# Flamingo block on one core: another order of the first two groups of rows

## The chip, the cores and the metric

The kernel runs on one core of a Trainium2 chip. The core has a matrix engine (PE, TensorE) with its weight loads (PEld), three engines for elementwise work (DVE or VectorE, ACT or ScalarE, POOL or GpSimd) and a queue engine (SP) that issues most transfers. Each engine takes its instructions in the order in which the program issues them, and waits on semaphores for what other engines and transfers produce. The metric is the device time of one execution in microseconds (us).

## The reference

Four batches of 2048 rows x of 512 columns; per batch a context of 77 rows of 384 columns. Everything is float32.

```
h  = layernorm(x);  q = h @ Wq;  k = ctx @ Wk;  v = ctx @ Wv      # 16 heads of 64
a  = softmax(q @ k.T / 8) @ v                                      # per batch and head
x  = x + tanh(g_xattn) * (a @ Wo + bo)
i  = argmax(log_softmax(logits) - log(-log(u)))                    # one of 8 weights
x  = x + tanh(g_ffn) * (layernorm(x) @ W[i] + b[i])
```

## The kernel before

**Weights are folded first.** Since a context has only 77 rows, q @ k.T is x @ M with M = centred Wq times K of a batch, and the attention's output is P @ VO with VO = V of a head times Wo. So per batch there is one M (512 x 1280, 16 heads by 80 padded keys) and one VO (1280 x 512). K (`project_k`, L274) and V (`project_v`, L278) come from the context, M from `m_head` (L298) and `build_m` (L310), VO from `build_vo` (L327), a pair of heads at a time. Batch 0's M stays in SBUF; the M of the other batches and every VO go to DRAM (`m_d`, `vo_d`) and are loaded when their batch comes (`load_m`, `load_vo`). A pair of VO takes six matmuls into six PSUM banks; `engines` in `build_vo` names the engine that copies each of them out ("D" DVE, "A" ACT, in turn) into one of five staging buffers `vo_st`, from which SP writes it to DRAM. Wo sits in the first part of the `vo` tile (L593), and three of the five staging buffers in its rest; the other two lie in the tile of Wq (L611).

**Rows go in 16 groups of 512.** Each group passes through scores (x @ M), softmax, attention (P @ VO), the residual, and the feed-forward with its own statistics. All products are done by a seven-product scheme (Strassen's, in Winograd's form): class `Seven` (L445). `product(s)` issues the matmuls of product s, `post(s)` takes the result out of PSUM: s = 0, 1, 2, 6 by a copy on ACT into `snap`, s = 3, 4, 5 by an addition on DVE (L486). A bank that collects several products is used again by a later product only after the post between them, so product 6 waits for post 4. The scheme needs sums of the blocks of each operand: `weight_sum` (L120) for M, VO and W; `Columns.sum` (L434) T1 to T4 of x's and P's columns, mostly on POOL. The scores of a group are three such runs: `s0` (two column pairs, snap), `s1` (two) and `s2` (one).

**Softmax.** DVE turns scores back to rows (`s_rows`, L512), takes a maximum per head group (`head_max`, L522, four of them), ACT does 64 exps of 128 x 77 (`exps`, L528), DVE sums (`head_sum`), POOL scales (`head_scale`, L542), and DVE turns P to columns (`p_columns`, L546, ten transposes). The layernorm of x enters as a scale of the exps: `Norms` (L358) with `stats` on DVE, `mean` and `var`, each a small DVE reduction (L374) followed by a small matmul (L375), and `rstd` with a power on POOL.

**Order by hand.** There is no scheduler: the program's text is each engine's order. The main loop (L756) runs for i = 1 to 15 and does the scores of group i, the attention of group i-1 with the exps of group i beside it, and the feed-forward of group i-1. Groups 0 and 1 have their scores written out ahead of it:

- L594 to L613, the setup: gates (L215: tanh of the gates, the choice of W[i]), then K and the centring of Wq per pair of heads, then M with V in its second and third quarter. Between them the statistics of group 0 and its columns. x is loaded behind all weights on SP.
- L649 to L697, scores of group 0. VO pairs 0 to 4 are made between its products: 0 and 1 in `s0`, 2 and 3 in `s1`, 4 at the end of `s2`. W[i] is gathered (L250) and centred (`centre_wf`, L621).
- L700 to L754, scores of group 1. VO 5 and 6 stand between its first products, VO 7 after the sixth; then `load_vo(0)`. Exps of group 0 and its sums are spread between. Only after all products come three VO weight sums on DVE and the ten transposes `p_columns(0, ...)` in two halves, then all ten `s_rows` of group 1.
- In the loop's first turn (i = 1) the attention of group 0 begins. There W[i] is scaled (`scale_wf`, L627, eight ACT instructions and four POOL sums) in its second step.

Of the kernel before, what the change touches and what calls it, by code (L numbers as in the profile page):

```python
# [8 lines left out]
F32 = mybir.dt.float32  # L9
# [5 lines left out]
P = 128  # L15
# [4 lines left out]
def flamingo_block_kernel(  # L20
# [33 lines left out]
    nc = tc.nc  # L54
# [60 lines left out]
    def flat(t):  # L115
        n = len(t.shape) - 1
        names = " ".join("abcdef"[:n])
        return t.rearrange(f"p {names} -> p ({names})")

    def weight_sum(w, n, engine=None):  # L120

        to, a, b_, op = ((5, 0, 3, ALU.subtract), (3, 3, 2, ALU.add), (4, 3, 0, ALU.subtract),
                         (6, 1, 4, ALU.subtract))[n]
        (engine or nc.gpsimd).tensor_tensor(flat(w[:, to]), flat(w[:, a]), flat(w[:, b_]), op)  # L124
# [12 lines left out]
        return wp.tile([P, NDC, T], F32, tag="xc", name=name, bufs=3)  # L137

    cT = wp.tile([P, NCC, B, JP], F32, tag="row", name="cT", bufs=3)
    cR = snap[:, : NCC * BJ].rearrange("p (c b j) -> p c b j", c=NCC, b=B)  # L140
    wv = snap.rearrange("p (c f) -> p c f", c=NCC)
    wk = m_f[:, 4 * 2 * KH * P :][:, : NCC * ID].rearrange("p (c f) -> p c f", c=NCC)
    t = wp.tile([P, NK * T + KH * T2], F32, tag="pT", name="wq")
# [16 lines left out]
    def load_w(t, w, h, queue):  # L160
        queue.dma_start(out=t[:, :, ts(h, ID // 4)], in_=w[:, ts(h, ID // 4)].rearrange("(c p) f -> p c f", p=P))

    nc.vector.memset(tq[:, 0], 0.0)
    idle = tq[:, 0].rearrange("p n t -> p (n t)")
    for _ in range(5):
        ps = bank("ps_w")
        nc.tensor.matmul(ps, idle[:, :P], idle, start=True, stop=True)
    load_ctx(0, nc.sync)
    load_ctx(2, nc.scalar)
    load_ctx(1, nc.sync)  # L170
    load_w(wk, Wk, 0, nc.scalar)
    load_w(wk, Wk, 1, nc.scalar)
    load_w(wk, Wk, 2, nc.sync)
    load_w(wk, Wk, 3, nc.sync)
    nc.gpsimd.memset(cT[:, :, :, J:], 0.0)
    for c in range(NCC):
        nc.vector.tensor_copy(cT[:, c, :, :J], cR[:, c])
    for p in range(NP):
        nc.sync.dma_start(out=wq[:, p, :], in_=WqT[ts(p, P), :])
    nc.gpsimd.dma_start(out=gg[:, 0:1], in_=g_xattn.partition_broadcast(P))  # L180
    nc.gpsimd.dma_start(out=gg[:, 1:2], in_=g_ffn.partition_broadcast(P))
    nc.gpsimd.dma_start(out=lg, in_=logits.partition_broadcast(P))
    nc.gpsimd.dma_start(out=uu, in_=u.partition_broadcast(P))
    for a in range(NA):
        nc.gpsimd.dma_start(out=bo_c[ts(a, 32)], in_=bo[ts(a, P)].rearrange("(q e) -> e q", e=32))
    for h in range(4):
        load_w(wv, Wv, h, nc.sync)
    load(0)
# [6 lines left out]
    for a in range(NA):  # L195

        for a2 in range(NA):
            nc.gpsimd.affine_select(
                out=jm[:, a, :], in_=jm[:, a, :], compare_op=ALU.not_equal, fill=0.125,
                base=-32 * a2, pattern=[[-1, 32]], channel_multiplier=1)  # L200

    def by_chunk(t):

# [60 lines left out]
    vT = [(vT_f[:, ts(p, BP)] if p < 7 else wf_f[:, ds(NP * BP, BP)]).rearrange(  # L264
        "p (r b k) -> p r b k", b=B, r=R) for p in range(NP)]

    def project(w, p):
        ps = bank("ps_kv")
        for c in range(NCC):
            nc.tensor.matmul(ps[:, :BP], w[:, c, ts(p, P)], cT[:, c].rearrange("p b j -> p (b j)"),  # L270
                             start=(c == 0), stop=(c == NCC - 1))
        return ps[:, :BP]

    def project_k(p):  # L274
        d = kT[:, p].rearrange("p b k r -> p (b k r)")
        nc.scalar.copy(d, project(wk, p))

    def project_v(p):  # L278
        d = vT[p].rearrange("p r b k -> p b k r")
        copy = nc.vector.tensor_copy if p % 2 else nc.scalar.copy  # L280
        copy(d, project(wv, p).rearrange("p (b k r) -> p b k r", b=B, r=R))


    wqp = [wp.tile([P, 2, NP, P], F32, tag="xc", name="wqp", bufs=3) for _ in range(2)]
# [2 lines left out]
    def centre_wq(p):  # L287
        nc.vector.tensor_reduce(wqm[:, p : p + 1], wq[:, p, :], AX.X, ALU.add)
        nc.vector.tensor_scalar(wqm[:, p : p + 1], wqm[:, p : p + 1], -1.0 / D, None, ALU.mult)
        for h in range(2):  # L290
            src = by_chunk(wq[:, p, :])[:, ts(h, 2)]
            dst = wqp[h][:, :, p, :].rearrange("p q (a e) -> p q a e", a=NA)
            if h:
                nc.gpsimd.tensor_scalar(dst, src, wqm[:, p : p + 1], None, ALU.add)
            else:
                nc.vector.tensor_scalar(dst, src, wqm[:, p : p + 1], None, ALU.add)
# [54 lines left out]

    def load_vo(bi):
        src = vo_d.rearrange("h (r b k) e -> (h r) b k e", b=B, k=NK)[:, bi]
        for (o, c), blk in BLK.items():
            nc.sync.dma_start(out=vo[:, blk], in_=src[:, ts(c, KH), ts(o, D // 2)])


    class Norms:  # L358
# [225 lines left out]
    def store(f, g0=0, n=NG, queues=(nc.sync,)):  # L584
        for a in range(NA):
# [2 lines left out]


    stages = [t[:, : (B - 1) * NK * P].rearrange("p (b k) -> p b k", b=B - 1) for t in  # L590
              (m_f[:, 4 * 2 * KH * P :], vo_f, vo_f[:, NP * D :],
               flat(wp.tile([P, HA, NG, JP], F32, tag="s", name="m_st")))]
    wo = vo_f[:, : NP * D].rearrange("p (n e) -> p n e", n=NP)  # L593
    norms[0] = Norms(0)  # L594
    gates()
    for p in range(NP):
        project_k(p)
        centre_wq(p)
    build_m(0, 0, NP // 2, stages[:2])
    norms[0].stats(xg[0], 0, 0, NG)  # L600
    build_m(0, NP // 2, NP, stages[:2], 0)
# [6 lines left out]
    build_m(2, NP // 2, NP, stages[2:])  # L608
    for n in range(1, 4):
        weight_sum(m, n, nc.gpsimd if n == 3 else nc.vector)  # L610
    for u_ in (vo_f[:, NP * D :], wq_f):  # L611
        for e in range(u_.shape[1] // (3 * D)):
            vo_st.append(u_[:, ts(e, 3 * D)].rearrange("p (c e) -> p c e", c=3))  # L613

# [12 lines left out]
    def scale_wf(wfr):  # L627
        for c in range(NDC):
            for o in range(2):
                nc.scalar.activation(chunked(wf[:, BLK[o, c // 2], c % 2, :]),  # L630
                                     by_chunk(wfr[:, c, :])[:, ts(o, 2)], AF.Copy, scale=tgf)
        for n in range(4):
            weight_sum(wf, n)

    def scores0(i):
        return Seven("ps_s", w_scores, xc[i], (0, 1), SNAP)
# [7 lines left out]
    def norm_step(n, s):  # L644
        if s < 4:
            (n.mean, n.spread, n.var, n.rstd)[s]()


    n = norms[0]  # L649
    s0 = scores0(0)  # L650
    for s in range(6):
        s0.product(s)
        if s == 0:
            wfr = gather()
        if s in (2, 5):
            build_vo(s // 3, "AD")
        s0.post(s)
    for k in range(2):
        s_rows(0, k, s0.chunk(0, k))
# [1 line left out]
    for s in range(7):  # L661
        s1.product(s)
        if s == 0:
            s1.post(0)
            s0.product(6)
            s0.post(6)
            for k in range(2):
                s_rows(0, KH + k, s0.chunk(1, k))
            sum_wf(wfr)
        else:  # L670
            norm_step(n, s - 1)
        if s in (2, 4):
            build_vo(1 + s // 2, "AD")
        if s == 3:
            x_columns(1)
        if 0 < s:
            s1.post(s)
        if s == 5:
            for k in range(2):
                s_rows(0, 2 + k, s1.chunk(0, k))  # L680
# [4 lines left out]
    for s in range(7):  # L685
        s2.product(s)
        s2.post(s)
        if s in (0, 2):
            n1.stats(xg[1], 0, 4 * s, 8)
        if s == 5:  # L690
            s_rows(0, 4, s2.chunk(0, 0))
            load(2)
            centre_wf(wfr)
            build_vo(4, "A")
    s_rows(0, KH + 4, s2.chunk(1, 0))
    for t in ("T1", "T2", "T3", "T4"):
        xc[1].sum(t)  # L697
# [4 lines left out]
    s1 = Seven("ps_s", w_scores, xc[1], (2, 3), pieces(spare, 0, 2))  # L702
    s2 = Seven("ps_s", w_scores, xc[1], (4,), SNAP1)
    head_max(0, 0)
    head_max(0, 1)
    for s in range(6):
        s0.product(s)
        s0.post(s)
        if s == 1:
            build_vo(5, "D")  # L710
            head_max(0, 2)
        if s == 3:
            build_vo(6, "D")
            head_max(0, 3)
        if s == 5:
            head_sum(0, 0)
            head_scale(0, 0)
        e = (0, 0, 8, 14, 20, 26, 32)
        exps(0, e[s], e[s + 1])
    build_vo(7, "D")  # L720
    load_vo(0)
    for s in range(7):
        s1.product(s)
        s2.product(s)
        if s == 0:
            s1.post(0)
            s2.post(0)
            s0.product(6)
            s0.post(6)
            head_sum(0, 1)  # L730
            head_scale(0, 1)
        norm_step(n1, s)
        if 0 < s:
            s1.post(s)
            s2.post(s)
        e = (32, 40, 48, 56, 64)
        if s < 4:
            exps(0, e[s], e[s + 1])
        if s == 2:
            head_sum(0, 2)  # L740
            head_scale(0, 2)
        if s == 4:
            head_sum(0, 3)
            head_scale(0, 3)
    weight_sum(vo, 0, nc.vector)
    p_columns(0, 0, 5)
    pT[0].sum("T1")
    weight_sum(vo, 1, nc.vector)
    weight_sum(vo, 2, nc.vector)
    p_columns(0, 5, NK)  # L750
    for sv, k0, nk in ((s0, 0, 2), (s1, 2, 2), (s2, 4, 1)):
        for half in range(2):
            for k in range(nk):
# [2 lines left out]
    for i in range(1, NGRP):  # L756
# [67 lines left out]
        for s in range(7):  # L824
# [12 lines left out]
            if 1 <= s:  # L837
                e = (0, 10, 20, 32, 44, 56, 64)
                exps(i, e[s - 1], e[s])
            if s == 0 and i == 1:  # L840
                weight_sum(vo, 3)
                pT[j].sum("T3")
            if s == 1 and i == 1:
                scale_wf(wfr)
            if s == 2:
                pT[j].sum("T4")
                if swap_m:
# [175 lines left out]
```

## Time and profile before

| what | us |
|---|---|
| median of 3 runs (1302.33 to 1303.58) | 1302.78 |
| the profiled execution | 1302.34 |
| its span, first to last instruction | 1300.4 |
| PE resumes after the statistics of group 0 | 33.27 |
| last matmul of M in the setup ends | 58.1 |
| group 0's scores, last product ends | about 106.4 |
| group 1's scores, last product ends | 148.57 |
| attention of group 0 begins | 151.26 |
| feed-forward of group 0 begins | 197.62 |

The page of the profile has the busy time of each engine and the span in 40 slices of 32.5 us. A timeline gives, for one engine, the start and length of instructions, merged where they follow each other, and in brackets the idle time before them with what ended it. A matmul of float32 shows as two records. Rows that serve below: a product of 4 matmuls in group 0's `s0` takes 1.73 us, an attention product (10 matmuls) 4.31, a VO pair 2.92 to 2.95; on DVE a head's maximum 1.44 and 0.17 for its scaling, a VO evacuation 0.66, a transpose 0.6 to 0.7; on ACT an exp 0.345, a VO evacuation 0.69; on POOL a sum of 128 x 1280 2.9, a head's scaling 2.27.

### The profile page before, as it was taken

The page shows a single profiled execution, that of the slowest core. Times are in us where ns is not written, and L with a number is a line of the kernel's source. Part 1 is how long each engine was busy: PE and PEld are TensorE (multiplying, and loading weights), DVE is VectorE, ACT ScalarE, POOL GpSimd, SP SyncE. Part 2 cuts the span into 40 slices and gives each one's busy share as a digit, 9 for nine tenths or more (in the row PEclk, how much of TensorE's full clock was granted, in tenths as well). Part 3 has the DMA queues.
Part 4 walks back from the last instruction along what each step waited for, and adds up shares of the span by engine and source line. Part 5 has one row for each costly group of instructions (what it writes and reads, how often), then busy time and mean ns, then how long its engine had stood idle before and what let it go on. Part 6 is the DMA issues. An engine that isn't in the chain of part 4 may idle for free.

```text
span 1300.4 us, 16961 instructions
## 1 busy us (share of the span) xinstructions
PE 1260.2 (97%) x5780; PEld 1068.9 (82%) x5780; DVE 884.8 (68%) x1823; ACT 651.6 (50%) x1766; POOL 894.2 (69%) x495
## 2 busy tenths in 40 slices
PE   9999869999999999999999999999999999999996
PEld 5666658888888888888888888888888888888885
DVE  6669776766667676766667676666767676666556
ACT  4436482644628273653728273563818264463822
POOL 5332478585977788585986788585985888585765
PEclk9999989999999999999999999999999999999998
DMA  9775310112305030022304120032304111010102
GB/s 237 254 254 160 116 33 1 37 29 81 65 1 121 26 65 1 18 48 81 66 1 106 41 55 12 3 64 74 73 1 99 48 35 31 1 33 1 33 1 65
DMA packets 95285, 80.28 MB, mean 62 GB/s; under 512 B 3920, under 2 KB 83152, under 8 KB 95200
## 3 DMA queue, kind: packets, MB, share of 16 engines
q1 hardware_dynamic: 92528, 76.61, 22.9%
q10 hardware_dynamic: 2064, 1.47, 0.4%
q0 software_dynamic: 608, 1.13, 0.4%
q8 instruction: 46, 0.75, 0.2%
q14 instruction: 39, 0.32, 0.1%
HBM read 44.07 MB, written 35.13 MB: 61 GB/s over the span
## 4 chain that ended last, share of the span: by engine, by line
PE 62%; ACT 14%; POOL 13%; DVE 6%; DMA 2%; issue 2%; SPq 0%; DVEq 0%; POOLq 0%; ACTq 0%
PE ps_s L463 36%; PE ps_a L463 16%; ACT s L532 12%; PE ps_f L463 7%; POOL xc L558 5%; POOL tq L437 4%; POOL s L543 4%; DVE sm L539 2%; PE ps_vo L336 1%; ACT snap L473 1%; PE ps_kv L270 1%; DMA xg<-in_x_dram 1%; DMA wq<-in_WqT_dram 1%; PE ps_m L301 1%; DVE s L515 1%
## 5 line engine op out<-in xcount | busy, mean ns | idle before, releaser
L463 PE MATMUL ps_a<-pT,vo 128*128 128x256 f32 x2240 | 491.2, 381 | 14.4 <-ACT snap L473 7.6
L463 PEld LDWEIGHTS ps_a<-pT,vo 128*128 128x128 f32 x2240 | 426.9, 191 | 75.3 <-POOL wf L124 7.9
L532 ACT ACTIVATE s<-s,nmx,up 128x77 f32<-128x77 f32 x1024 | 355.7, 446 | 6.0 <-DVE nmx L526 6.0
L463 PE MATMUL ps_s<-tq,m 128*128 128x256 f32 x1280 | 294.1, 380 | 0.2 <-DVE m L124 0.2
L437 POOL TENSOR_TENSOR pT<-pT 128x1280 f32<-128x1280 f32 x64 | 186.8, 2920 | 131.7 <-PE ps_a L463 111.3
L463 PEld LDWEIGHTS ps_s<-tq,m 128*128 128x128 f32 x1280 | 241.6, 190 | 35.0 <-issue 2.4
L469 ACT COPY snap<-ps_s 128x512 f32<-128x512 f32 (+1 forms) x188 | 94.4, 511 | 310.4 <-DVE t L417 124.2
L463 PE MATMUL ps_s<-xc,m 128*128 128x256 f32 x960 | 222.9, 381 | 0.6 <-DVE wq L339 0.6
L463 PEld LDWEIGHTS ps_s<-xc,m 128*128 128x128 f32 x960 | 180.8, 190 | 28.9 <-DVE wq L339 2.3
L543 POOL TENSOR_TENSOR s<-s,sm 128x1232 f32<-128x1232 f32 x64 | 145.2, 2268 | 73.9 <-DVE sm L540 64.6
L486 DVE TENSOR_TENSOR snap<-snap,ps_s 128x512 f32<-128x512 f32 (+1 forms) x141 | 83.6, 594 | 91.3 <-PE ps_s L463 91.3
L515 DVE STREAM_TRANSPOSE s<-snap 128x512 f32<-128x512 f32 x156 | 100.0, 686 | 49.3 <-ACT snap L469 47.4
L539 DVE TENSOR_REDUCE sm<-s 128x16 f32<-128x1232 f32 x64 | 91.7, 1432 | 56.8 <-ACT s L532 56.8
L463 PE MATMUL ps_f<-tq,wf 128*128 128x256 f32 x512 | 120.3, 383 | 8.0 <-POOL tq L437 8.0
L578 ACT ACTIVATE t<-t,rs 128x128 f32<-128x128 f32 x248 | 75.8, 390 | 98.7 <-POOL rs L409 98.7
L463 PEld LDWEIGHTS ps_f<-tq,wf 128*128 128x128 f32 x512 | 95.7, 190 | 27.5 <-POOL tq L437 15.2
L402 POOL TENSOR_TENSOR rs<-rs,neghalf 128x16 f32<-128x16 f32 x16 | 50.2, 3136 | 93.6 <-DVE rs L399 93.6
L552 DVE STREAM_TRANSPOSE pT<-s 128x512 f32<-128x512 f32 x160 | 101.0, 678 | 13.8 <-POOL s L543 13.8
L437 POOL TENSOR_TENSOR tq<-xc,tq 128x512 f32<-128x512 f32 x64 | 81.5, 1273 | 32.6 <-PE ps_f L463 25.6
L473 ACT ACTIVATE snap<-ps_a,bo_c 128x256 f32<-128x256 f32 x128 | 53.7, 470 | 90.0 <-PE ps_a L463 54.4
L437 POOL TENSOR_TENSOR tq<-xc 128x512 f32<-128x512 f32 x64 | 81.3, 1270 | 24.1 <-DVE xc L412 18.1
L524 DVE TENSOR_REDUCE ps_st<-s 128x16 f32<-128x1232 f32 x64 | 92.4, 1444 | 2.1
(121 smaller groups left out, 1200.9 us busy)
## 6 DMA issues: line engine op xcount, KB each, us to landing
xg<-in_x_dram SPq DMA_DIRECT2D x64, 256.0 KB, 5.6
out_dram<-y SPq DMA_DIRECT2D x60, 256.0 KB, 4.0
vo<-vo_d SPq DMA_DIRECT2D x16, 640.0 KB, 5.4
m<-m_d SPq DMA_DIRECT2D x12, 640.0 KB, 3.9
vo_d<-vo SPq DMA_DIRECT2D x10, 512.0 KB, 3.4
m_d<-vo SPq DMA_DIRECT2D x4, 960.0 KB, 8.0
vo_d<-wq SPq DMA_DIRECT2D x6, 512.0 KB, 2.8
wq<-in_WqT_dram SPq DMA_DIRECT2D x8, 256.0 KB, 8.1
```

Of the source, the lines that this page charges most:

```text
L437: (engine or nc.gpsimd).tensor_tensor(self.at[name], self.at[a], self.at[b_], op)
L463: nc.tensor.matmul(self.ps[r][:, n, :], self.w(blk, c, pair), self.cols(cname, c), start=(first and n == 0 and c == 0), stop=(c == h - 1), ...
L469: nc.scalar.copy(dst, self.ps[r])
L473: nc.scalar.activation(dst[:, n, :], self.ps[r][:, n, :], AF.Identity, scale=1.0, bias=self.bias[:, q : q + 1])
L486: nc.vector.tensor_tensor(c, c, self.ps[r], ALU.add)
L515: nc.vector.transpose(key_chunk(sc[i], k), cols.rearrange("p (g h r) -> p g h r", h=HA, r=R))
L524: nc.vector.tensor_reduce(mx, head(i, h), AX.X, ALU.max)
L532: nc.scalar.activation(head(i, h)[:, g, :], head(i, h)[:, g, :], AF.Exp, scale=norms[i].up[:, g : g + 1], bias=nmx[h][:, g : g + 1])
L539: nc.vector.tensor_reduce(sm, head(i, h), AX.X, ALU.add)
L543: nc.gpsimd.tensor_tensor(head(i, h), head(i, h), sums[h].unsqueeze(2).to_broadcast([P, NG, J]), ALU.mult)
L552: nc.vector.transpose(pT[i].all[:, k, :].rearrange("p (g h r) -> p g h r", h=HA, r=R), key_chunk(sc[i], k))
L578: nc.scalar.activation(ts_[f][:, g, :], ts_[f][:, g, :], AF.Copy, scale=rs[:, g : g + 1])
```

## The change

The diff moves work between the setup and the first two groups; the loop for groups 2 and on is the same.

1. Setup. The context is loaded raw into the tile that later stages M (`s_f`) instead of `snap`, and K reads it there with 77 columns per batch; only V reads the padded copy. POOL zeroes K's padding. Three warm-up matmuls instead of five. Wk's second quarter is issued on SP and its third on ACT, instead of the other way round. POOL's constants come ahead of the loads of the gates' inputs; the gates are computed after three of the eight K pairs; the bias `bo` is loaded after the loop.
2. VO. Pair 0 ahead of group 0's scores, 1 and 2 inside `s0`; 3 and 4 ahead of group 1's scores, 5 to 7 after its first three products. Evacuations "AAD" for pair 0, "AD" for 1 and 2, "ADD" for 3 to 7. The staging buffers in Wq's tile are used first. `load_vo(0)` follows VO 7, its blocks in another order.
3. W[i] is centred and scaled inside `s2` of group 0; three of its four sums are in `s1` and `s2` of group 1, the fourth in the attention.
4. The statistics of group 1 (`norm_step`) move from `s1`, `s2` to `s0` of group 1; exps and sums of group 0 are spread anew; eight of the ten `p_columns` and POOL's T1 move into steps 3 to 5 of `s1`, `s2`; the three VO weight sums move from DVE to POOL.

```diff
-    cR = snap[:, : NCC * BJ].rearrange("p (c b j) -> p c b j", c=NCC, b=B)
+    s_f = flat(wp.tile([P, HA, NG, JP], F32, tag="s", name="m_st"))
+    cR = s_f[:, : NCC * BJ].rearrange("p (c b j) -> p c b j", c=NCC, b=B)
...
-    for _ in range(5):
+    for _ in range(3):
...
     load_w(wk, Wk, 0, nc.scalar)
-    load_w(wk, Wk, 1, nc.scalar)
-    load_w(wk, Wk, 2, nc.sync)
+    load_w(wk, Wk, 1, nc.sync)
+    load_w(wk, Wk, 2, nc.scalar)
     load_w(wk, Wk, 3, nc.sync)
...
-    nc.gpsimd.dma_start(out=gg[:, 0:1], in_=g_xattn.partition_broadcast(P))
...
     nc.gpsimd.memset(jm, 0.0)
     for a in range(NA):
         for a2 in range(NA):
             nc.gpsimd.affine_select(
...
+    nc.gpsimd.dma_start(out=gg[:, 0:1], in_=g_xattn.partition_broadcast(P))
...
+    kT_f = kT.rearrange("p n b k r -> p n b (k r)")
+    nc.gpsimd.memset(kT_f[:, :, :, J:], 0.0)
...
     def project_k(p):
-        d = kT[:, p].rearrange("p b k r -> p (b k r)")
-        nc.scalar.copy(d, project(wk, p))
+        nc.scalar.copy(kT_f[:, p, :, :J], project(wk, p, cR).rearrange("p (b j) -> p b j", b=B))
...
     norms[0] = Norms(0)
-    gates()
     for p in range(NP):
+        if p == 3:
+            gates()
         project_k(p)
         centre_wq(p)
+    for a in range(NA):
+        nc.gpsimd.dma_start(out=bo_c[ts(a, 32)], in_=bo[ts(a, P)].rearrange("(q e) -> e q", e=32))
...
-    for u_ in (vo_f[:, NP * D :], wq_f):
+    for u_ in (wq_f, vo_f[:, NP * D :]):
...
     n = norms[0]
+    build_vo(0, "AAD")
     s0 = scores0(0)
...
         if s in (2, 5):
-            build_vo(s // 3, "AD")
+            build_vo(1 + s // 3, "AD")
         s0.post(s)
...
-        if s in (2, 4):
-            build_vo(1 + s // 2, "AD")
...
             n1.stats(xg[1], 0, 4 * s, 8)
+        if s == 1:
+            centre_wf(wfr)
+        if s == 3:
+            scale_wf(wfr)
         if s == 5:
             s_rows(0, 4, s2.chunk(0, 0))
             load(2)
-            centre_wf(wfr)
-            build_vo(4, "A")
...
     head_max(0, 0)
+    build_vo(3, "ADD")
     head_max(0, 1)
+    exps(0, 0, 6)
+    build_vo(4, "ADD")
+    head_max(0, 2)
+    exps(0, 6, 10)
+    e = (10, 16, 22, 28, 35, 42, 48)
     for s in range(6):
         s0.product(s)
         s0.post(s)
-        if s == 1:
-            build_vo(5, "D")
-            head_max(0, 2)
-        if s == 3:
-            build_vo(6, "D")
+        if s < 3:
+            build_vo(5 + s, "ADD")
+        if s == 0:
             head_max(0, 3)
-        if s == 5:
-            head_sum(0, 0)
-            head_scale(0, 0)
-        e = (0, 0, 8, 14, 20, 26, 32)
+        norm_step(n1, s)
         exps(0, e[s], e[s + 1])
-    build_vo(7, "D")
-    load_vo(0)
+        if s == 2:
+            load_vo(0)
+        if s in (2, 4):
+            head_sum(0, s // 2 - 1)
+            head_scale(0, s // 2 - 1)
+    e = (48, 53, 58, 64)
     for s in range(7):
         s1.product(s)
         s2.product(s)
...
-            head_sum(0, 1)
-            head_scale(0, 1)
-        norm_step(n1, s)
+            head_sum(0, 2)
+            head_scale(0, 2)
+            weight_sum(wf, 0)
+        if s < 3:
+            exps(0, e[s], e[s + 1])
+        if s == 1:
+            weight_sum(wf, 1)
+            weight_sum(wf, 2)
+        if s == 2:
+            head_sum(0, 3)
+            head_scale(0, 3)
+        if 3 <= s < 6:
+            p_columns(0, (0, 3, 5)[s - 3], (3, 5, 8)[s - 3])
+        if s == 4:
+            pT[0].sum("T1")
+        if s == 5:
+            weight_sum(vo, 0)
         if 0 < s:
             s1.post(s)
             s2.post(s)
...
-    weight_sum(vo, 0, nc.vector)
-    p_columns(0, 0, 5)
-    pT[0].sum("T1")
-    weight_sum(vo, 1, nc.vector)
-    weight_sum(vo, 2, nc.vector)
-    p_columns(0, 5, NK)
+    p_columns(0, 8, NK)
+    weight_sum(vo, 1)
+    weight_sum(vo, 2)
...
             if s == 0 and i == 1:
+                pT[j].sum("T3")
                 weight_sum(vo, 3)
-                pT[j].sum("T3")
-            if s == 1 and i == 1:
-                scale_wf(wfr)
+                weight_sum(wf, 3)
```

## The prediction, on record before the changed kernel ran

> **What bounds the kernel now.** I read the page's first two parts, then the matrix engine's (PE) timeline, then busy time by ten microseconds, then the timelines of the other engines and of the DMA queue SP, and last the order in which the changed kernel puts instructions on each engine.
>
> ```profile
> PE 1260.2 (97%) x5780; PEld 1068.9 (82%) x5780; DVE 884.8 (68%) x1823; ACT 651.6 (50%) x1766; POOL 894.2 (69%) x495
> PEclk9999989999999999999999999999999999999998
> ```
>
> PE is the bound, so only PE's own gaps can be won, and the clock fell only in the sixth slice of 32.5 us. From group 2 on PE hardly waits, and the change leaves those groups alone. The gaps stand before 210 us:
>
> ```profile
> 127.36 2.86 PE L463 MATMUL ps_s<-xc,m 128*128 128x256 f32 x12 [0.64 <-DVE wq L339]
> ...
> 151.26 5.18 PE L463 MATMUL ps_a<-pT,vo 128*128 128x256 f32 x20 [2.69 <-issue]
> 157.71 4.58 PE L463 MATMUL ps_a<-pT,vo 128*128 128x256 f32 x20 [1.26 <-POOL pT L437]
> 165.13 8.90 PE L463 MATMUL ps_a<-pT,vo 128*128 128x256 f32 x40 [2.84 <-POOL pT L437]
> 181.59 16.19 PE L463 MATMUL ps_a<-pT,vo 128*128 128x256 f32 x60 [7.57 <-ACT snap L473]
> 197.62 1.89 PE L463 MATMUL ps_f<-xc,wf 128*128 128x256 f32 x8
> ```
>
> Columns: start, length, what, and in brackets the wait. The waits shown make 15.0 us; 0.21, 0.36, 0.37 and 0.40 at 60, 81, 132 and 205 us make 16.3. After the 7.57 us wait the clock is low. One microsecond at a time:
>
> ```profile
> 176.00:177.00 1.00, 0.00 (x0) 1.00 0.00 0
> 177.00:178.00 1.00, 0.00 (x0) 0.72 0.00 0
> 178.00:179.00 1.00, 0.00 (x0) 0.50 0.00 0
> ...
> 186.00:187.00 1.00, 1.00 (x4) 0.50 0.00 0
> 187.00:188.00 1.00, 1.00 (x5) 0.66 0.00 0
> ```
>
> The fourth number is the granted clock: half from 177.4, 3.4 us after the last matmul (174.0), to 187.7. PE ran at half for 6.1 us (181.6 to 187.7) and lost 3.0. All told 19.3 us can be won, 1283 if nothing is added. DVE sits in front of these waits:
>
> ```profile
> 147.57 2.97 DVE L124 TENSOR_TENSOR vo<-vo 128x1280 f32<-128x1280 f32 x1
> 150.47 3.07 DVE L552 STREAM_TRANSPOSE pT<-s 128x512 f32<-128x512 f32 x5
> 153.47 5.54 DVE L124 TENSOR_TENSOR vo<-vo 128x1280 f32<-128x1280 f32 x2
> 158.93 3.07 DVE L552 STREAM_TRANSPOSE pT<-s 128x512 f32<-128x512 f32 x5
> ```
>
> Two of DVE's three VO weight sums (8.5 us in all) stand between the halves of P's transposes; the score transposes (6.2), the maxima, and on ACT exps and W's scaling (3.2) queue up behind.
>
> **The change part by part.** I follow one chain to the start of group 0's feed-forward, 197.62 before.
>
> *Setup: nothing.* Two warm-up matmuls go, keys read 308 columns instead of 320 (12/320 of 13.3 us, 0.5), Wk's second quarter moves to SP (0.64 wait at 12.5). All of it ends under one cover: DVE's statistics of x wait for x's landing at 29.5, and PE resumes at 33.27 behind them. The gates now stand in the key loop, and their small loads start some 5 us later on POOL (4.05 us of selects, plus memsets, come first). The logits took 7.8 us to land, so they come at about 15; gates 4.6, five centrings at 1.17 and eight pairs of copies at 0.47 bring DVE to 29.3. Without cover: between -0.5 (x sooner) and +3 (loads at 9.3, the slowest bias landing, and cold matmuls); I take +0.4, nearest to the logits' row.
>
> *VO 0 ahead of all scores: +2.6.* PE takes it in order, right behind the M heads (end 58.1), and it needs Wo:
>
> ```profile
> 51.67 0.37 SPq L605 DMA_DIRECT2D vo<-in_Wo_dram x1
> ```
>
> It landed after 9.2 us, so at 60.9 (it waits for M's writes, which don't move). PE waits 2.8 where it waited 0.2.
>
> *Group 0's scores: +2.1.* From 60.9, by rows: three VO pairs at 2.95, six products at 1.75, seven more to the sixth of the second run, and the statistics (0.6): 93.2. Then DVE: add 0.7, four transposes 2.6 with a wait of 0.3, two batches of statistics 3.2, the centring of W 2.44, three adds 1.07. The second of the adds ends at 103.2 and PE's last product needs it. PE is there at 101.05; before, VO 4 stood in this spot as cover. W's scaling on ACT (3.3) fits beside. The product, ACT's copy and two transposes bring DVE to 105.2, PE to 104.1.
>
> *VO 3 to 5 ahead of and in group 1's scores: +5.2, the largest new wait.* The order shows PE's mean of group 1's statistics now behind VO 5, and DVE's reduction for it behind the fourth maximum. DVE has from 105.2 four maxima at 1.66, twelve evacuations at 0.66 and 0.15: 14.75, to 119.95. PE has three VO pairs and one product, 10.5, to about 114.75. Behind the waiting matmul stand all other products; ACT finishes exps 0 to 15 and waits for a product too. Bounds 3.5 to 6: evacuations between 0.65 and 0.74, maxima between 1.57 and 1.76.
>
> *VO 6, 7 and the rest.* PE: 0.15, 1.75, 2.95, 1.75, 2.95, to 129.5, and 0.9 for the second mean, whose reduction follows VO 7's evacuation. ACT leaves VO 7 at 129.3 with 42 exps to do: 14.5 at 0.345, copies 2.3, 0.9 waiting for a product: 147.1. Before, exps ended at 145.0. Head sum 1.7 and POOL's scaling 2.3: P's transposes start at 151.2 (before: 150.47). Five of them and two adds later, 155.4, POOL can begin; PE is held 2.9 by the adds between.
>
> *Attention of group 0: the gain.* POOL does T1, three VO sums and T2 in a row, 14.55 at 2.91; the third product starts at 170.0 (waits of 1.1 and 1.5 within). Five products at 4.31 follow: 191.5. ACT no longer holds W's scaling; exps of group 1 start behind DVE's ten score transposes at 168.6, and 20 of them with two copies end at 177.2, before the fifth product at 178.6. So the 7.57 us wait and its half clock go. The vo loads are issued at about 132, landing in 4.4, covered until 155.
>
> *Feed-forward: +1.9.* The other 44 exps end 0.9 behind PE's last product; before they ended 1.1 ahead. POOL's scaling of the third head, two residuals and T1 then end at 194.7 where PE wants T1 at 193.2 (1.5), and T3 costs 0.8 instead of 0.4. Bounds 0 and 3.
>
> Sum: 191.5 + 1.9 = 193.4, against 197.62: -4.2; with setup -3.8. On the profiled execution's 1302.34 (span 1300.4 and 1.9 around it) that is 1298.5; the median of the runs, 1302.78, lies 0.44 above, so 1299.0 as a median.
>
> **A rule against the trace.** The trace has waits of 2.69 and 2.84 us at full clock and one fall, 3.4 us into the 7.57. The new wait of 5.2 lies between. If the fall comes as it did, PE runs at half for some 6 us after 120 and loses 3.0 (bounds 0 and 3.4); ACT and DVE hang on PE's products there, so all of it is paid. One fall doesn't tell whether 3.4 us is a fixed delay, so I give the fall a little under even odds.
> The Trainium skill, "TensorE: Matmul & The Clock Gate", Part 1 ("What's actually happening"), says that the clock halves after a whole idle window of about 3.4 us, and that these windows run freely. By it an estimate is that a 5.2 us wait holds a whole window about every second time; the sum is then 1299 in one half of the executions and 1302 in the other, where the row alone, read as a fixed delay, gives 1302 in all. The same page wants some 3.4 us of matmuls to warm up, which speaks against leaving out two; x's landing covers most of that.
>
> **Rivals.**
> *The clock falls in the new wait:* 1302.0. For it: 5.2 exceeds 3.4. Against: the phase may differ, and the last VO 5 tiles may wait for banks and shorten the gap.
> *The new waits are mostly covered:* if DVE is 2 us earlier in group 0's last scores (103.2 is the sum of nine rows, each with an overlap that I may miss) and exps come as early as in before's ordering, waits of 2.1, 2.9, 2.6 and 1.9 go: 1290. Against: they come from queue orders, not from durations.
> *Slower: VO's writes don't land.* Five staging buffers serve two per pair; VO 5's second head takes the buffer of VO 3's first, written out from 108.2 and wanted at 115.5. VO writes land in 3.4 us (median), up to 9.0. VO 3 and 4 (1.31 MB each) and x of group 2 (1.05) now move in 10 us, 367 GB/s, where the busiest four microseconds showed 393. From 7.2 us of landing on, DVE waits; at 11 the wait is 3.8 longer, 9.0 in all, the clock falls as it did after 7.57, and the time is 1299 + 3.8 + 3.0 = 1305.8.
> *The gates come late:* setup +3 instead of +0.4, 1301.6; with the clock's fall 1304.6.
> That the change doesn't do what it says is excluded: the order of each engine shows the moves.
>
> **How the numbers follow.** Forecast 1299 (own range 1296 to 1301): 0.38. Clock falls, 1302 (1300 to 1304): 0.26. Waits covered, 1290 (1284 to 1296): 0.14. Writes late, 1305.8 and above: 0.14. Gates late, 1301.6 to 1306: 0.08. 0.2%, or 2.6 us, is about what a measurement of this kernel can tell from no change. Faster (under 1300.2): 0.35 of the first, 0.04 of the second, all of the third: 0.53. Slower (over 1305.4): the writes' case and half of the gates': 0.18. Same: 0.29. The range 1290 to 1305 leaves out half of the covered case and most of the writes': some 0.2.
>
> **What would show it.** PE idle until about 61 ahead of the first VO matmul; the last score product of group 0 waiting 2 us for a DVE add; one PE wait of about 5 us on a reduction near 115, and its clock there; exps ending near 147; waits on POOL between the first three attention products; the third wave of exps without a wait of 7 us. Wrong would be: Wo landing before 58, DVE ahead of PE at the mean, or a setup that resumes after 34.

## The result and the profile after

The changed kernel takes 1305.37 us (median of 14 runs, 1302.66 to 1307.29) against 1302.79 (14 runs, 1302.00 to 1304.95) beside it: 1.0019 times as long, 95% interval 1.0010 to 1.0027. That is 6.4 us above the forecast of 1299.0, just outside the forecast's range of 1290 to 1305, and slower than before where it was to be faster. The runs also lie further apart than before: 4.6 us against 3.0.

The profiled execution took 1304.32 us (span 1302.5). The timeline of the matrix engine (PE) of the changed kernel, with the places that the prediction named (start, length, what, and in brackets the wait and what ended it):

```profile
61.79 3.08 PE L339 MATMUL ps_vo<-vo,wq 64*128 64x512 f32 x12 [3.04 <-DMA vo<-in_Wo_dram]
104.72 1.95 PE L466 MATMUL ps_s<-tq,m 128*128 128x256 f32 x4 [2.09 <-DVE snap L489]
122.34 0.61 PE L378 MATMUL ps_st<-tot,jm 128*128 128x16 f32 x2 [4.16 <-DVE tot L377]
122.79 3.76 PE L466 MATMUL ps_s<-tq,m 128*128 128x256 f32 x8
137.03 0.39 PE L378 MATMUL ps_st<-tot,jm 128*128 128x16 f32 x2 [1.58 <-DVE tot L377]
162.71 4.54 PE L466 MATMUL ps_s<-tq,m 128*128 128x256 f32 x12 [2.74 <-DVE sn L489]
176.81 21.85 PE L466 MATMUL ps_a<-pT,vo 128*128 128x256 f32 x100 [0.93 <-POOL pT L440]
198.50 1.89 PE L466 MATMUL ps_f<-xc,wf 128*128 128x256 f32 x8
```

Before's waits of 2.84 and 7.57 us in the attention are gone, as forecast, and the new waits are where they were forecast. But read the lengths. Eight score matmul records last 3.76 us at 122.79, where eight like them last 1.99 us at 130.53 and 113.27. The clock is at half there. The view by microsecond (length, PE busy with its count, granted clock, DMA):

```profile
121.00:122.00 1.00, 0.00 (x0) 0.98 1.07 336
122.00:123.00 1.00, 0.66 (x3) 0.50 0.92 242
127.00:128.00 1.00, 1.00 (x4) 0.50 0.00 0
128.00:129.00 1.00, 1.00 (x4) 0.61 0.00 0
```

A microsecond at 0.98 was at half speed for 0.04 of it, so the fall is at 121.96 and, from the 0.61, the return at 128.79. Read in the same way, the clock is at half in three more stretches: 26.38 to 29.79, 104.88 to 108.29 and 162.92 to 166.33. Each of the four begins in one of the waits or just behind it (3.46 in M's heads, 2.09, 4.16, 2.74), and each lasts 3.41 us or twice that. In the last three PE has about 13.3 us of work at half speed, which is 6.6 us lost. Feed-forward of group 0 starts at 198.50 instead of the forecast 191.5.

All edges lie on one grid: from 104.88, five steps of 3.413 give 121.95, seventeen give 162.90. PE's busy time in the grid's windows just ahead of the three falls:

```profile
101.47:104.88 3.41, 1.32 (x7) 1.00 0.00 0
118.55:121.96 3.41, 0.00 (x0) 1.00 0.94 329
159.51:162.92 3.41, 0.67 (x4) 1.00 0.00 0
```

PE was busy for 39%, 0% and 20% of them. Only one window was idle throughout. The same grid in the trace of before (fall at 177.44) puts its wait of 2.69 us across a boundary, 1.57 us on one side and 1.12 on the other, and its wait of 2.84 as 1.50 and 1.34: no window is idle for over half, and there was no fall. **Theory A**: the clock is set at the ends of windows of 3.413 us that run on whatever the kernel does, and halves when PE was idle for more than about 60% of one; waits from some 2.1 us up can do it, and the phase decides. **Rival B**: the waits themselves cost the time. **Rival C**: it is lost elsewhere, in setup or later. The prediction's own reading (a fall some 3.4 us after the last matmul) is **rival D**.

### The profile page after: what moved, and what is told of

The parts are those of the page before. It is cut to its first block, busy times and chain, and to the rows that moved or that the text cites. A ratio compares the mean times of both kernels' runs of the same rounds, so it can differ in the third digit from the quotient of the medians.

```text
span 1302.5 us, 16960 instructions
## 1 busy us (share of the span) xinstructions
PE 1261.0 (97%) x5776; PEld 1071.9 (82%) x5776; DVE 875.4 (67%) x1818; ACT 652.8 (50%) x1768; POOL 901.8 (69%) x499
## 4 chain that ended last, share of the span: by engine, by line
PE 58%; POOL 13%; ACT 13%; DVE 4%; issue 1%; POOLq 0%; DVEq 0%; ACTq 0%
PE ps_s L466 34%; PE ps_a L466 16%; ACT s L535 12%; PE ps_f L466 7%; POOL xc L561 5%; POOL s L546 4%; POOL tq L440 4%; DVE sm L542 2%; ACT snap L476 1%; PE ps_vo L339 1%; DVE s L518 0%; PE ps_st L378 0%; DVE pT L555 0%; DVE sm L543 0%; DVE y L986 0%
## 5 line engine op out<-in xcount | busy, mean ns | idle before, releaser
L466 PE MATMUL ps_s<-tq,m 128*128 128x256 f32 x1280 | 298.3, 384 | 4.8 <-DVE sn L489 2.7
L466 PEld LDWEIGHTS ps_s<-tq,m 128*128 128x128 f32 x1280 | 244.3, 192 | 39.9 <-DVE sn L489 3.1
L466 PE MATMUL ps_f<-tq,wf 128*128 128x256 f32 x512 | 120.4, 383 | 8.6 <-POOL tq L440 8.6
```

The lines of the kernel that those rows point to most:

```text
L466: nc.tensor.matmul(self.ps[r][:, n, :], self.w(blk, c, pair), self.cols(cname, c), start=(first and n == 0 and c == 0), stop=(c == h - 1), ...
```

## The experiments

| kernel | median us | ratio to before, 95% | feed-forward starts (profile) |
|---|---|---|---|
| before | 1302.79 | | 197.62 |
| changed | 1305.37 | 1.0010 to 1.0027 | 198.50 |
| fill_after | 1301.23 | 0.9981 to 0.9999 | 197.62 |
| fill_all | 1299.91 | 0.9973 to 0.9991 | 193.47 |
| fill_before | 1302.70 | 0.9992 to 1.0010 | 195.15 |
| setup_only | 1302.92 | 0.9993 to 1.0011 | 197.60 |
| rest_only | 1303.41 | 1.0002 to 1.0020 | 196.74 |
| mean_early | 1301.41 | 0.9983 to 1.0001 | 195.16 |
| all_fix | 1294.32 | 0.9920 to 0.9947 | 192.28 |
| best | 1300.70 | 0.9976 to 0.9995 | 196.09 |
| best2 | 1291.39 | 0.9901 to 0.9929 | 186.76 |

Each ratio is to the kernel before as it ran beside that kernel; its medians were 1302.40 to 1302.79, so differences between rows of the table carry up to 0.4 us from that. All rows are medians of 11 runs, but for all_fix and best2 (5 each) and the first two (14).

### Waits kept, clock kept: fill_after and fill_all

```
+    def filler(n):
+        ps = bank("ps_w")
+        for _ in range(n):
+            nc.tensor.matmul(ps[:, :T2]..., ones, ones.unsqueeze(1).to_broadcast([P, 2, P]), ...)
...
+        if s == 6:
+            filler(4)          # ahead of s2.product(6) of group 0
...
+        if s == 0:
+            filler(9)          # ahead of n1.mean()
...
+        if s == 6:
+            filler(6)          # ahead of s1.product(6) of group 1
```

> The changed kernel with matmuls of a constant into a spare bank put ahead of three of the matrix engine's waiting matmuls (4 ahead of group 0's last score product, 9 ahead of group 1's first statistics matmul, 6 ahead of group 1's last score product, 0.43 us each): the waits stay as long as they were, and the engine is busy in them. Theory A (the time is lost to falls of the granted clock that waits of 2.1, 4.2 and 2.7 us set off): the half clock at 105, 122 and 163 us is gone, about 6.6 us less, 1297.5 to 1300. Rival B (only the waits themselves cost; the half clock lies beside other work): 1305, none won, up to 0.5 more where filling runs past the wait. Rival C (the loss is elsewhere: setup, later groups): 1305 too.

1301.23 us, 4.1 below the changed kernel (3.9 with each taken against its own before): B and C, which had 1305, are out, for nothing was shortened. It is less than A's 6.6 and misses A's 1297.5 to 1300, and the runs still spread over 6 us (1299.11 to 1305.12). The trace of one of the slower executions (1303.61) shows a reason: the three falls are gone, but here the clock fell at 63.2 us, in VO 0's wait for Wo, whose matmuls then took 4.68 us instead of 3.08:

```profile
63.22 4.68 PE L339 MATMUL ps_vo<-vo,wq 64*128 64x512 f32 x12 [3.04 <-DMA vo<-in_Wo_dram]
```

In the changed kernel's profile the same wait of 3.04 us lay across a boundary of the grid and cost no clock. And in M's heads the clock stayed low for two windows instead of one. So the other waits were filled too:

> As fill_after, and filled also in the 3.5 us wait of setup (9 matmuls ahead of M's 11th head), in VO 0's wait for Wo (7) and in the wait of 1.6 us ahead of the second statistics matmul (3). Theory A (falls of the clock, wherever the phase of the grid puts them): no half clock between 20 and 200 us, 1297 to 1300, and a spread of the runs no wider than that of the kernel before (3 us), where the changed kernel and fill_after had 5 to 6. Rival B (fill_after won by something else than the clock): no better than fill_after's 1301.2, with its spread.

1299.91 us with a spread of 2.4 us, both as A says. Its timeline around the longest wait, and the granted clock by 25 us (its own, then the changed kernel's):

```profile
103.61 1.13 PE L473 MATMUL ps_s<-tq,m 128*128 128x256 f32 x4 [0.36 <-DVE snap L496]
115.55 4.15 PE L657 MATMUL ps_w<-ones 128*128 128x256 f32 x18
120.42 0.39 PE L385 MATMUL ps_st<-tot,jm 128*128 128x16 f32 x2 [0.71 <-DVE tot L384]
```

```profile
100.00:125.00 25.00, 23.92 (x104) 1.00 0.49 158
125.00:150.00 25.00, 24.91 (x114) 1.00 0.82 241
150.00:175.00 25.00, 22.49 (x102) 1.00 0.08 12
```

```profile
100.00:125.00 25.00, 18.75 (x68) 0.87 0.48 158
125.00:150.00 25.00, 23.42 (x97) 0.92 0.65 215
150.00:175.00 25.00, 22.26 (x96) 0.93 0.25 38
```

The matmul on the statistics still has to wait for VectorE (DVE), from 115.5 to 120.4; PE only passes the time in work that nobody needs. It is not this execution alone: the mean granted clock is 0.996 or 0.997 in all 11 runs of fill_all, and in the 14 of the changed kernel it goes from 0.991 in the fastest to 0.987 in the slowest. 1305.37 less 1299.91, 5.5 us, is what the falls cost in the median (5.1 with each taken against its own before).

### The same filling in the kernel before: fill_before

```
         for s in range(7):
+            if s == 4 and i == 1:
+                filler(16)
             at.product(s)
```

> The kernel before with 16 matmuls of a constant (6.9 us) in its 7.57 us wait ahead of the fifth attention product of group 0, so that the wait stays and the engine is busy. Theory A: the half clock from 177.4 to 187.7 us goes and with it 3.0 us: 1299.5 to 1300.5. Rival B: 1302.8, no change.

A, as I stated it, missed here: 1302.70, no gain. The clock did stay up in the profiled execution, and the timeline shows where the 3 us went:

```profile
182.12 13.19 PE L463 MATMUL ps_a<-pT,vo 128*128 128x256 f32 x60 [0.66 <-ACT snap L473]
195.15 1.89 PE L463 MATMUL ps_f<-xc,wf 128*128 128x256 f32 x8
199.58 3.72 PE L463 MATMUL ps_f<-tq,wf 128*128 128x256 f32 x16 [2.54 <-POOL tq L437]
```

The three attention products take 13.19 us instead of 16.19, and then PE waits 2.54 us for GpSimd's (POOL's) T1 of the feed-forward. The runs agree: one of mean clock 0.997 took 1302.45 us, one of 0.994 took 1302.46. Half a clock costs what it delays, not what it slows: here, beside a later chain on another engine, it was free. In the changed kernel it wasn't, since ScalarE's (ACT's) exps and all behind them hung on the slowed products: the last exp ends at 153.87 there and at 148.82 in fill_all.

### The parts by themselves: setup_only and rest_only

setup_only is before with the diff's hunks on loads, warm-ups, keys and gates; rest_only is before with all other hunks.

> The kernel before with the change's setup alone (context read uncopied, 3 warm-ups, order of the Wk quarters, POOL's loads behind its constants, gates in the key loop); the rest as before. The prediction's step: +0.4, 1303.0. Theory A: the gates put a wait of some 3.5 us into M's heads, whose half clock of one or two windows delays the scores by 0.6 to 2.3 us, not covered by x: 1303.2 to 1305. Rival: nothing, 1302.6, since POOL's chain covers it before the feed-forward.

> The kernel before with the change's new order of groups 0 and 1 alone, and the old setup. Theory A: falls of the clock behind the waits of 2.1, 4.2 and 2.7 us as in the changed kernel, setup's 0.6 to 2.3 us gone: 1302.5 to 1305. If setup were free: 1305.4.

setup_only 1302.92, 0.47 above the before of its runs; the forecast step was +0.4, and A's 1303.2 to 1305 is missed. rest_only 1303.41, 0.96 above, within A's bounds; its trace has the changed kernel's three falls, at 103.1, 120.2 and 161.1, in or behind waits of 2.08, 4.19 and 2.74 us, and none in setup. The two sum to 1.4, less than the whole's 2.6, but the intervals are about 1.1 us to each side, so that isn't settled. More is to be seen in setup_only's trace. It has before's waits of 2.69 and 2.83 us (2.84 there):

```profile
151.65 11.03 PE L466 MATMUL ps_a<-pT,vo 128*128 128x256 f32 x40 [2.69 <-issue]
165.52 10.59 PE L466 MATMUL ps_a<-pT,vo 128*128 128x256 f32 x40 [2.83 <-POOL pT L440]
```

The granted clock behind both, first in the trace of before, then in setup_only's:

```profile
153.00:154.00 1.00, 1.00 (x5) 1.00 0.00 0
166.00:167.00 1.00, 1.00 (x7) 1.00 0.00 0
```

```profile
153.00:154.00 1.00, 1.00 (x4) 0.55 0.00 0
166.00:167.00 1.00, 1.00 (x5) 0.88 0.00 0
```

In before it stays full; here it falls behind both, at 153.10 and 166.76, four windows apart. The same wait in another phase of the grid: this is what the prediction's trace of one execution could not show. (And it cost nothing: the feed-forward starts at 197.60, since the wait that was 7.57 us is only 5.88.)

### The disputed rule by itself: ladder and ladder64

Behind the end of the changed kernel, bursts of matmuls with a DVE add of n columns between:

```
+    for n in (500, 2000, 1250, 3000, 750, 2250, 1500, 1000, 2500, 1750, 2750) * 3:
+        nc.vector.tensor_tensor(m_f[:, ds(P, n)], snap[:, :n], snap[:, :n], ALU.add)
+        ps = bank("ps_w")
+        for _ in range(24):
+            nc.tensor.matmul(ps[:, :T2], ones, m_f[:, ds(P, T2)], start=True, stop=True)
```

> The changed kernel, and behind its end 33 bursts of 24 matmuls (about 10.3 us each) with waits of about 0.8 to 3.6 us between them, eleven lengths three times, set by one add of 500 to 3000 columns on VectorE. Theory A (the clock is decided at the ends of windows of 3.41 us on a running grid, and halves where a window was idle for some 60% or more): no fall after waits under 2.0 us, some after 2.1 to 3.3 us according to where the wait lies in the grid, all falls 3.41 us or a multiple of it apart. Rival D (a wait has to last a whole 3.4 us): no fall, or only after the longest. Rival E (a fixed length of wait, counted from the last matmul): every wait above one length falls, none below, whatever the phase.

A burst at full clock lasts 10.63 us; longer ones lost clock. From the timeline, five of the 33:

```profile
1420.88 10.63 PE L997 MATMUL ps_w<-m,ones 128*128 128x256 f32 x48 [2.08 <-DVE m L994]
1528.85 10.63 PE L997 MATMUL ps_w<-m,ones 128*128 128x256 f32 x48 [1.81 <-DVE m L994]
1554.26 10.63 PE L997 MATMUL ps_w<-m,ones 128*128 128x256 f32 x48 [2.86 <-DVE m L994]
1566.96 12.30 PE L997 MATMUL ps_w<-m,ones 128*128 128x256 f32 x48 [2.08 <-DVE m L994]
1700.71 13.68 PE L997 MATMUL ps_w<-m,ones 128*128 128x256 f32 x48 [2.86 <-DVE m L994]
```

Waits of 2.08 and of 2.86 us come out both ways. Up to 1.91 us none of 14 waits made the clock fall; at 2.1, 2.3, 2.6, 2.9 and 3.1 us 2, 2, 2, 1 and 2 of three did; at 3.4 us three of three. All edges of this stretch lie within 0.03 us of one grid of 3.413 us. On that grid the most idle window without a fall was idle for 56%, the least idle window with one for 60%. D and E are out. Two windows of other runs show that the limit is not a sharp one in PE's busy time. The four in order are the ladder's two, then one of setup_only, then one of mean_early (below):

```profile
1549.91:1553.32 3.41, 1.49 (x7) 1.00 0.00 0
1659.14:1662.55 3.41, 1.37 (x6) 1.00 0.00 0
149.69:153.10 3.41, 1.45 (x5) 1.00 0.00 0
155.19:158.60 3.41, 1.41 (x7) 1.00 0.00 0
```

The second and third were followed by a fall, the first and fourth were not: with PE busy for 1.41 and 1.45 us of a window both came out. The return: a burst of the ladder lost 1.7 us (one window) when the window behind the fall was idle for at most 7%, and some 3 us (two) when it was idle for 18% or more. Windows behind falls in mean_early and in the changed kernel narrow that:

```profile
25.48:28.90 3.42, 3.09 (x12) 0.50 1.22 201
121.96:125.37 3.41, 3.03 (x8) 0.50 0.68 213
```

Behind the first, 10% idle, the clock came back; behind the second, 11% idle, it did not.

ladder64 is the same with matmuls of 64 contracted rows (`ones[:64], m_f[:64, ...]`) and shorter waits.

> As ladder, with matmuls that contract 64 rows instead of 128, and waits of some 0.4 to 2.9 us (adds of 100 to 2500 columns). Theory A1 (the clock asks only for how long the matrix engine was busy in a window): falls as in ladder, none below 2.0 us. Theory A2 (it asks for the rows at work, and 64 count half, so that a busy share of some 84% is needed): falls after waits from 0.6 us up, wherever they lie in one window; it would also tell why all_fix fell with 46% idle in a window of VO matmuls, and ladder not with 56%.

Neither answer came as expected, because the clock never came back at all. Its view by stretches:

```profile
1310.00:1500.00 190.00, 178.43 (x412) 0.50 0.00 0
1500.00:2000.00 500.00, 466.75 (x1075) 0.50 0.00 0
```

PE was busy for 93% of 690 us and stayed at half. In the ladder, whose matmuls differ in the rows alone, it came back behind every full window. So the rows at work do count, in the return at least, as far as one run shows; whether they count in the fall this run can't say, as the bursts never had a full clock to lose.

### One wait taken out, and four: mean_early and all_fix

```
+    n1.mean()
     head_max(0, 0)
     build_vo(3, "ADD")
...
-        norm_step(n1, s)
+        norm_step(n1, s + 1)
```

> The changed kernel with group 1's mean issued ahead of the four maxima and each later step of its statistics one product earlier; nothing else. Theory A: the wait of 4.2 us and its half clock over two windows (3.2) go, a wait for the later step of up to 2 us comes: 1299.5 to 1302.5. Rival B (the wait alone): 1302 to 1304. Rival F (ACT's exps or POOL's sums set the end whatever PE does there): 1305, no change.

1301.41, 4.0 below the changed kernel (3.6 with each against its own before): inside A's bounds and 0.6 us below B's (the interval is 1.2 to each side, so this run alone would not decide). The wait of 4.16 is gone; 1.28 stays in its place and the second statistics matmul waits 2.25 instead of 1.58, so the waits alone gave 2.2 us. In the profile the clock is at half in two stretches on this path (from 104.0 and from 127.9); behind the wait of 2.74 us, where it fell in the changed kernel and in rest_only, it stays full here.

all_fix has that edit and three more, ahead of VO 0, of group 0's last score product and of group 1's:

```
-    build_vo(0, "AAD")
     s0 = scores0(0)
...
+        if s == 1:
+            build_vo(0, "AAD")
...
             load(2)
+            build_vo(3, "ADD")
...
     head_max(0, 0)
-    build_vo(3, "ADD")
...
+        if 0 < s:
+            s1.post(s)
+            s2.post(s)
         if 3 <= s < 6:
             p_columns(0, (0, 3, 5)[s - 3], (3, 5, 8)[s - 3])
...
-        if 0 < s:
-            s1.post(s)
-            s2.post(s)
```

> The changed kernel with the four waits taken out by order: VO 0 behind the second score product, VO 3 ahead of group 0's last score product, group 1's mean ahead of the maxima (each later step of its statistics one product earlier), and the adds of group 1's last products ahead of the transposes of P in the same step. Theory A: waits of 3.0, 2.1, 4.2 and 2.7 us and 6.6 us of half clock are up to 18.6 us; some returns as a wait for the exps and for POOL's sums, which follow the same chain: 1288 to 1295. Rival B: the waits alone, 12 us less what returns: 1294 to 1299. Rival C: within 2 us of 1305.

1294.32, 11.0 below the changed kernel and 8.3 below before. Both A's bounds and B's hold it, so this run doesn't decide between them. Two falls stay on the path, behind

```profile
124.18 0.40 PE L378 MATMUL ps_st<-tot,jm 128*128 128x16 f32 x2 [1.58 <-DVE tot L377]
164.59 27.85 PE L466 MATMUL ps_a<-pT,vo 128*128 128x256 f32 x120 [3.19 <-POOL vo L124]
```

The first doesn't fit the ladder: the window up to 124.74 was idle for 46% only. Its busy part is VO matmuls (64 rows, the last of them 64 columns wide) and statistics of 16 columns, so it may have counted for less; that is open.

### A version that beats both: best, then best2

Both are all_fix with each statistics matmul of group 1 issued one VO behind its reduction (so that its operand should be there when PE meets it) and `filler(6)` ahead of group 0's second attention product. best also has POOL's loads ahead of its constants again, and nine constant matmuls in M's heads; in best2 the second maximum of group 0 comes behind the first statistics matmul, in best ahead of it. The cut is of best.

```
+    n1.mean(False)             # the reduction alone
     head_max(0, 0)
...
     build_vo(4, "ADD")
+    n1.matmul()                # its matmul
...
+        if s == 0:
+            n1.spread()
+            n1.var(False)
+        if s == 1:
+            n1.matmul()
+            n1.rstd()
...
         for s in range(7):
+            if s == 1 and i == 1:
+                filler(6)
             at.product(s)
```

> As all_fix, and: POOL's small loads ahead of its constants again (the gates without their wait for the logits), each statistics matmul of group 1 issued one VO behind its reduction, and constant matmuls in two waits that stay (9 in M's heads, 6 ahead of group 0's second attention product). Theory A: the waits of 2.3 and 1.6 us and the falls of all_fix at 25, 125 and 166 us go; POOL's sums behind the exps set the end, which come some 3 to 4 us sooner: 1289 to 1292. Rival F (exps and sums follow another chain): 1293 to 1294.5, as all_fix.

A miss: 1300.70. The setup lines of its timeline:

```profile
28.35 1.53 PE L304 MATMUL ps_m<-wf,wqp 64*128 64x320 f32 x4 [5.80 <-DVE vo L311]
29.81 6.29 PE L334 MATMUL ps_st<-ones 128*128 128x256 f32 x18
```

WqT now landed at 13.67 instead of 9.69, so that DVE's copies came later, PE was stopped three heads sooner, and the nine constant matmuls stood behind the wait, at half clock, for 6.3 us of PE's own path: scores started at 66.97 instead of all_fix's 60.46. A filler is free only inside the wait. The loss lies ahead of the scores: from there to the feed-forward best takes 129.1 us, all_fix 131.8. But the split did not do there what it was meant to. The first statistics matmul, which shares a tile with DVE's maxima, now waited for the second of them, longer than all_fix's 2.26 us, and the clock fell at 119.5:

```profile
118.20 0.40 PE L391 MATMUL ps_st<-tot,jm 128*128 128x16 f32 x2 [2.71 <-DVE nmx L542]
```

> all_fix, with the changed kernel's setup as it is, each statistics matmul of group 1 issued one VO behind its reduction, and 6 constant matmuls in the wait ahead of group 0's second attention product. If best lost its time in setup alone (its nine constant matmuls came behind the wait, at half clock, and held M's heads for 6.3 us): the waits of 2.3 and 1.6 us and two falls of all_fix go, 1289 to 1292. If splitting the statistics is what cost it: 1294 or more.

1291.39 us, 0.9915 times before (0.9901 to 0.9929), 11.0 us less, by order and six spare matmuls. The first statistics matmul still waits 1.01 us for a maximum, the second not at all. Half clock is left only in setup, in M's heads, and the feed-forward starts at 186.76.

## Why the prediction was wrong

- **The step that failed is the clock.** The prediction held one fall possible, in the wait of "5.2", at "a little under even odds" and 3.0 us, and took it into a rival (1302.0); in the forecast's sum the clock costs nothing. It read "waits of 2.69 and 2.84 us at full clock" as waits too short to matter. setup_only shows the clock fall behind these same two waits, the ladder shows falls from 2.08 us up, and the changed kernel had three on its path, two of them behind waits of 2.09 and 2.74 us. fill_all, with the waits kept, takes 1299.91: 5.1 to 5.5 of the 6.4 us that were missed are clock.
- **The waits themselves were right, within about 1 us.** Wo: 3.04 (forecast 2.8). Group 0's last score product: 2.09 (about 2.1). The mean: 4.16 (5.2, bounds 3.5 to 6); DVE's run of maxima and evacuations took 14.4 us (14.75). The second mean: 1.58 (0.9). The last score product of group 1: 2.74 (2.9). Third attention product: 0.93 in the changed kernel and, at full clock in fill_all, 1.11 and 1.25 (1.1 and 1.5).
- **The chain to the feed-forward:** 193.47 in fill_all (191.5). Most of the 2.0 us is there when P's transposes start: 153.02 (151.2). Of that, ACT's run of exps behind VO 7 is 0.9, 18.7 us where the rows gave 17.8; the rest lies ahead of it.
- **The half clock of before was no gain to be had in that kernel.** The prediction put 3.0 us of its 19.3 that "can be won" on it. fill_before won none: POOL's T1 comes up behind it. In the sum it did no harm, since that sum follows the chain and has the feed-forward's waits in it (+1.9; in fill_all +0.55: 0.95 us in two waits, 0.40 before). That this term was 1.35 us too large hid two thirds of the chain's 2.0: luck.
- **Setup**, +0.4: +0.47 by itself in setup_only (interval -0.9 to +1.4), +0.6 in the changed kernel's profile (M's heads end at 58.75, before 58.12). The agreement is luck: the wait of 3.46 us and the half clock in M's heads weren't foreseen. With the clock kept, in fill_all, M's heads end at 57.5, sooner than before; with two windows of half clock, in fill_after and all_fix, at 60.2 and 60.5.
- **Rivals.** VO's writes came in time: DVE shows no wait for a buffer in its run after 107.9. "Mostly covered" didn't happen. The gates' place did put a wait into M's heads, but at +0.6 us of its +3. The clock's rival was the right mechanism with one fall where the path had three, 3.0 us where they cost 5.1 to 5.5.
- **The page.** The Trainium skill, "TensorE: Matmul & The Clock Gate", Part 1 ("What's actually happening"), has the clock watched in free-running windows of 3413 ns; the ladder's grid of 3.413 us agrees with it. It has the clock halve after a whole idle window; here windows idle for 57% (setup_only), 60% (ladder) and 61% (the changed kernel) were enough, though one of 59% in mean_early was not, and the measurement decides. By the page's rule I put a fall in the 5.2 us wait at about every second time; by the 60% of these runs a wait of over 4.1 us makes the clock fall in any phase, since of two neighbouring windows one holds at least half of it (2.05 us).

## What to carry to other kernels

Cost a new wait of the matrix engine of some 2 us or more as the wait and, by its chance, half a window to a whole one (1.7 to 3.4 us) of lost clock. An estimate from the ladder's grid and limit: a wait w between 2.05 and 3.4 us covers 60% of a 3.413 us window in about (w - 0.7)/3.4 of the phases (over the ladder's 15 waits of 2.1 to 3.1 us that makes 8.4 falls; 9 came). One execution's trace shows one phase. Several such waits on one path made the time longer and its spread wider here (4.6 us, and 2.4 with the waits filled). Splitting a reduction from the matmul that reads it, so that other matmuls stand between, took one such wait out in best2 and left 1.01 us of the other's 2.26. And price a half clock by what hangs on the slowed matmuls: ahead of a chain on another engine that ends later, as in fill_before, it cost nothing.

## What the runs showed of the hardware that was not expected

- The clock halved at the end of a 3.413 us window with PE busy for up to 43% of it (setup_only, 1.45 of 3.41 us; 54% in all_fix's open case), and returned only behind a window that was all but full: 10% idle sufficed (mean_early), 11% did not (the changed kernel).
- Matmuls of 64 contracted rows, one behind the other on the same 64, never brought the clock back: 0.50 for over 700 us of bursts of 20.8 us with waits of 0.4 to 2.9 us between. VO's and M's matmuls of 64 rows, which alternate between the two halves, ran at full clock for 6 us at a stretch, and a window of M's matmuls alone, 26.38 to 29.79 in the changed kernel, brought it back.
- A small change in the order of loads went with a late large one: with four loads of 0.5 to 4 KB ahead on POOL's queue, WqT's first quarter megabyte landed 4 us later (13.67 in best; 9.69 in the changed kernel, 10.27 in all_fix). One execution each; the cause was not tried.
